# A three-layer graph convolution: two teams for three in the second layer, four blocks more fetched by index, a longer landing ring

## The chip, the core and the metric

The kernel runs on one core of one Trainium2 chip. The metric is the device time of one execution in microseconds, median of several runs. A core has five engines with a queue each: TensorE (PE in the profile, its weight loads PEld), VectorE (DVE), ScalarE (ACT), GpSimd (POOL) and SyncE (SP, here used for starting DMAs). An engine works through its queue in order.

## The reference

A graph has N = 6250 nodes with 256 features and 100,000 edges, sorted by destination. Three graph-convolution layers follow each other, then a residual and a layer norm:

```python
deg  = segment_sum(1, dst with self loops);  dinv = rsqrt(deg)
h = x
for W, b in ((W1, b1), (W2, b2), (W3, b3)):       # 256 -> 512 -> 512 -> 256
    t   = h @ W
    agg = segment_sum(t[src] * (dinv[src] * dinv[dst]), dst)
    h   = relu(agg + b)
return layernorm(x + h)
```

## The kernel before, in words

The nodes lie in 50 blocks of 125 (`NB`, `Q`). For each layer a table in HBM holds one row per node, scaled by `dinv` (`tab0`, `tab1`, `tab2`; rows of the second are 512 floats, 2 KB). A block's aggregate is the sum over the edges that end in it, and the kernel has two ways to it.

*By fetched rows.* The block's edges stand in 16 groups of 128 (`KF`), and an edge list of leftovers serves ten blocks together (`rest`). For a group, GpSimd starts an indirect DMA that fetches 128 rows (`gather`); TensorE multiplies them with a 0/1 matrix made by VectorE (`more_hots`). For two passes of fast matmuls each fetched row is split into a rounded high part (a cast on ScalarE) and the rest (a subtraction on VectorE).

*By count matrices.* The first layer makes, for 29 blocks, a matrix of 125 x 6250 edge counts and keeps it in HBM (`kept`). A block's aggregate is then 50 products of a count piece with a block of the table. In the first and third layer these stand under `L1398`; in the second layer four blocks form a team (`teams`): the table is streamed from HBM in pairs of blocks, split into two parts, and multiplied with count pieces that are 500 columns wide. One turn of the inner loop is a pair, two matmuls of 500 columns (L1004). A team takes 50 x 4 pairs.

`layer(i, ...)` writes out one layer by hand: its loop runs over `chunk`, one fetched group per turn (called a step below). In each step it issues the gather of group c, the cast of group c - `hi_lag`, the subtraction of group c - `lo_lag`, the two matmuls of group c - `lag`, and then lets other coroutines go on: `going` holds the dense stages behind finished blocks (`after2`, `hidden`: L1417, L1504, L1512, L1524, L1539 and so on), `fixed` holds the extras: `teams`, `in_advance` (the third layer's first products, for three blocks) and `home`. A coroutine that yields n is called again n steps later. The order in each engine's queue is just the order of this code.

In the second layer the 12 team blocks are blocks 0 to 11; blocks 12 to 49 are fetched, 38 x 16 groups and 4 of leftovers, 612 steps. Fetched rows land in `wide_rows`, eight places of 2 KB in `room` and `back`, one of them for leftovers. Split rows lie in nine places and three lent ones (`loaned`) in the big tile `all_parts`; until the teams are done, the part of `all_parts` behind block `HOME` serves as the teams' working space (`carved`): stream ring, count pieces, both parts. Finished blocks of the third table whose place in `parts` lies there go only to HBM (`waiting`), and `home` reloads them after the teams, in runs of up to four. `returning` is set six units before the teams end; from then on the loans go back and the lags shrink. `PACE` sets how the teams' pairs follow from step 9 (`EAGER`) on.

Of the kernel before, what the change touches and what calls it, by code (L numbers as in the profile page):

```python
# [10 lines left out]
F32 = mybir.dt.float32  # L11
# [15 lines left out]
Q = 125  # L27
KF = 16
# [10 lines left out]
SPLIT_ROWS = (12, 9, 20)  # L39
LOANED = 3  # L40
EAGER = 9
PACE = 24
LANDING = 8
AT_ONCE = 3
RETURN = 6
SHORT = 6
# [9 lines left out]
BOTH_LAG = 5  # L56
SPLIT = ((0, 0, BOTH_LAG), (1, 2, 8), (0, 0, 10))
EXTRAS_AFTER = (3, 6, 9, 11, 13, 15, 17)
TEAM = 4
TEAMS = 3  # L60
HOME = 17
TAIL = 4
MANY = 29
BEGUN = 3
SOONER = -2
ADVANCE = (0, 12, 17, 22, 27, 32, 37)
AT_HOME = 2
ALONE = 2
# [339 lines left out]
def sorted_path(ctx: ExitStack, tc: tile.TileContext, x, edges, starts, found, wts, biases, room, late, out):  # L408
# [347 lines left out]
    x_rows = [room[:Q, 3 * MW:3 * MW + C], scratch[:Q, MW:MW + C]]  # L756
    turn = 0

# [141 lines left out]

    RING = 3
    streamed = [carved(2 * HID).bitcast(F32).rearrange("p (b c) -> p b c", b=2) for _ in range(RING)]
# [5 lines left out]
    loaned = [wide_tail[:, cut - n * 2 * HID:][:, :2 * HID] for n in range(LOANED, 0, -1)]  # L908
    on_loan = []
    team_banks = [accs[2], mat_bank, mm_bank, tr_bank]  # L910
    couple, waiting = [], []
# [3 lines left out]
    def teams(groups):  # L915
# [71 lines left out]
        for u, (g, k) in enumerate(units):  # L987
            if u == len(units) - RETURN:
                returning = now
            if u % 2:  # L990
                load((u + 1) // 2 + RING - 1)
            for n in range(TEAM):
                if k == 0:
                    yield from take(f"team{n}", 1)
                if k == NB - 1 and n == 0:
                    while held.get("tz", 0):
                        yield 1
                    held["tz"] = TEAM // 2
                if 1 <= n < 3:
                    half(u + 2, n - 1)  # L1000
                if k % PIECE == 2 and u + PIECE < len(units):
                    piece(*divmod(g * CUTS + k // PIECE + 1, CUTS), n)
                for h in range(2):
                    nc.tensor.matmul(team_banks[n][:, :TEAM * Q], lhsT=both_parts[u % 3][:, h * HID + n * P:h * HID + (n + 1) * P],  # L1004
                                     rhs=team_pieces[(g * CUTS + k // PIECE) % 2][:, k % PIECE, :],
                                     start=(k == h == 0), stop=(k == NB - 1 and h == 1))
                if k == NB - 1:
                    team_ended[0](scaled(g, n))
                pairs_done += 1
                if in_layer == 0 and pairs_done % 3 or in_layer == 1 and (pairs_done % PACE if now >= EAGER else pairs_done % 3 == 0):  # L1010
                    yield 1
# [14 lines left out]
    def in_advance():  # L1026
# [36 lines left out]
        for u, (m, k0) in enumerate(units):  # L1063
# [3 lines left out]
            for k in range(PIECE):  # L1067
# [3 lines left out]
                sent += 1  # L1071
                if sent % (2 if u < AT_HOME * BEGUN else AT_ONCE):
                    yield 1

    def home():
# [9 lines left out]
        for run in runs:  # L1085
            b, e = run[0], run[-1] + 1
            by_rows(nc.sync, parts[:, b:e].bitcast(F32), tables[2][b * Q:e * Q, :].rearrange("(b p) c -> p b c", p=Q))
            final.update((k, now + LANDING) for k in range(b, e))
            yield 4

# [65 lines left out]
    def layer(i, width, gathered, dense, after, rows, first=0, spacing=1.0, extras=(), carried=None):  # L1156
# [6 lines left out]

        nonlocal turn, finished, now, in_layer, products
        in_layer = i
# [101 lines left out]
        def of_both(c):  # L1267

            n, b, _ = items[c]
            return i == 2 or i == 0 and (n * GRP if b is None else b) >= BOTH_FROM  # L1270

        def halved(c):

# [8 lines left out]
        def gather(c):  # L1282
            nonlocal turn
            n, b, j = items[c]
# [12 lines left out]
            else:  # L1297
                row, at = rows[turn % len(rows)], src[:, b, j:j + 1]
                (landed if i == 1 else split_rows)[c] = row
                turn += 1  # L1300
            nc.gpsimd.indirect_dma_start(out=row, out_offset=None, in_=table,  # L1301
# [43 lines left out]
        with tc.manual_schedule():  # L1345
            more_hots()
            to_sum = 0
            for chunk in range(total + (SHORT if i == 1 else lag)):
# [3 lines left out]
                if i == 1:  # L1352
                    lag = SPLIT[i][2] if returning is None else max(SHORT, SPLIT[i][2] - (chunk - returning) // 2)
                if chunk < total:
                    gather(chunk)
                if halved(chunk - hi_lag):
                    halves = split_rows[chunk - hi_lag] = split.popleft()
                    if i == 1 and halves in loaned:
                        on_loan.append(halves)
                    nc.scalar.copy(halves[:, :width], landed[chunk - hi_lag])  # L1360
                if halved(chunk - lo_lag):
                    halves = split_rows[chunk - lo_lag]
                    nc.vector.tensor_sub(halves[:, width:], landed.pop(chunk - lo_lag), halves[:, :width].bitcast(F32))  # L1363
                while to_sum <= chunk - lag:
# [57 lines left out]
    def after1(b, acc, bank):  # L1422
# [28 lines left out]
        nc.scalar.activation(y, y, AF.Relu, scale=dinv[:, b:b + 1])  # L1451
        by_rows(nc.sync, y, tables[1][b * Q:(b + 1) * Q, :], store=True)

# [186 lines left out]
    def last_weights():  # L1640
# [9 lines left out]
    own_row = two.enter_context(tc.tile_pool(name="sown_row", bufs=1)).tile([P, HID], F32, name="own_row")[:Q]  # L1650
    layer(1, HID, every[TEAM * TEAMS:], [], after2, wide_rows,
          extras=[(5, last_weights()), (0, team_steps), (20, in_advance()), (20, home())])
    there[:] = [0]
# [193 lines left out]
```

## Time and profile before

| | |
|---|---|
| Time, median of 3 runs | 2064.19 us (2059.42 to 2065.3) |
| Profiled execution | 2065.68 us, its span 2063.9 us |
| Mean granted TensorE clock | 0.984 |
| HBM traffic | 459.56 MB read, 73.87 MB written, 258 GB/s over the span |
| First gather of the second layer | at 709.7 us |
| Last gather of the second layer | at 1616.9 us |
| First gathers of the third layer | just before 1650 us |

The profile's lines name a source line (L1301 is the gather in `layer`), the engine, the operation, the tiles written and read, the count, the busy time and mean duration, and then the engine's idle time just before such instructions with the releaser that ended most of it. The releaser "issue" means that the profile shows nothing that was waited for. Matmuls overlap each other, so that the mean of one is longer than its share of the engine's time; the shares are read from busy time by stage. A gather's duration is the time in which GpSimd makes the DMA; the rows land later. Fetched rows in the second layer have `room` or `back` as their tile (after the change also `parts`); in the third layer, `halves`.

### The profile page before, as it was taken

How to read it: one execution, taken by the hardware profiler on the slowest of the kernel's cores; microseconds unless marked ns; L12 is line 12 of the kernel's file. 1: busy time of each engine (PE TensorE's matmuls, PEld its weight loads, DVE VectorE, ACT ScalarE, POOL GpSimd, SP SyncE). 2: the span in 40 equal slices, each digit the busy share in tenths (PEclk: the TensorE clock that was granted, in tenths of full speed). 3: DMA queues.
4: the chain of work that ended last, by engine and by line, in shares of the span. 5: the costliest groups of instructions: out<-in, count | busy, mean ns of one | idle time of the engine just before them, and what ended most of it. 6: DMA issues, size and time to landing. Idle time of an engine off the chain costs nothing.

```text
span 2063.9 us, 29139 instructions
## 1 busy us (share of the span) xinstructions
PE 1925.4 (93%) x8679; PEld 1517.8 (74%) x8679; DVE 1377.3 (67%) x2443; ACT 1278.4 (62%) x2255; POOL 1383.6 (67%) x1425
## 2 busy tenths in 40 slices
PE   4499999999999689999999989999989999999997
PEld 3377777777777467778888768887768777778776
DVE  6877888888882277777676676766756445444444
ACT  2566777787875366666676666666656455555553
POOL 2466777766777377677777676766657277777775
PEclk9999999999999899999999999999999999999999
DMA  7898999999999999999999998989897599999997
GB/s 172 247 293 227 265 264 259 273 262 255 276 273 250 258 267 262 264 261 267 261 258 263 264 261 250 268 252 258 248 272 234 151 286 290 290 298 295 294 285 204
DMA packets 266078, 535.53 MB, mean 259 GB/s; under 512 B 44363, under 2 KB 80328, under 8 KB 265910
## 3 DMA queue, kind: packets, MB, share of 16 engines
q0 software_dynamic: 155280, 355.58, 63.0%
q1 hardware_dynamic: 97348, 168.71, 30.5%
q10 hardware_dynamic: 13282, 9.30, 1.7%
q8 instruction: 70, 1.15, 0.2%
q14 instruction: 98, 0.80, 0.1%
HBM read 459.56 MB, written 73.87 MB: 258 GB/s over the span
## 4 chain that ended last, share of the span: by engine, by line
PE 62%; DMA 13%; issue 9%; POOL 8%; DVE 3%; ACT 2%; SPq 0%; POOLq 0%; DVEq 0%; ACTq 0%
PE sacc L1329 12%; DMA room<-tab,ssrc 6%; PE win_ps L1398 6%; PE str L1398 5%; PE smm L1398 5%; PE sacc L1398 5%; PE mat_ps L1398 5%; POOL room L1301 5%; PE win_ps L1504 4%; PE win_ps L1524 2%; POOL back L1301 2%; DMA back<-tab,ssrc 2%; PE sacc L1443 2%; DMA parts<-tab 2%; PE sacc L877 1%
## 5 line engine op out<-in xcount | busy, mean ns | idle before, releaser
L1301 POOL DMA_INDIRECT room<-tab,ssrc x442 | 456.3, 1032 | 201.6 <-issue 82.5
L1329 PE MATMUL sacc<-halves,shot 128*125 128x512 f32 x1524 | 517.2, 400 | 10.3 <-ACT halves L1360 3.9
L1254 ACT CAST piece<-room 125x625 fp32r<-125x625 uint8 x492 | 350.7, 720 | 186.7 <-PE win_ps L1398 52.7
L1301 POOL DMA_INDIRECT halves<-both,ssrc x384 | 360.7, 939 | 144.3 <-issue 42.7
L1301 POOL DMA_INDIRECT halves<-tab,ssrc x320 | 302.9, 947 | 97.8 <-issue 22.0
L1329 PEld LDWEIGHTS sacc<-halves,shot 128*125 128x125 f32 x1524 | 284.9, 187 | 87.0 <-DVE halves L1363 8.2
L810 DVE TENSOR_TENSOR back<-near_cols,slots 128x625 bf16<-128x625 f32 (+2 forms) x435 | 325.0, 803 | 29.7 <-PE sacc L877 13.0
L1363 DVE TENSOR_TENSOR halves<-room,halves 128x512 fp32r<-128x512 f32 x334 | 227.1, 693 | 126.0 <-ACT halves L1360 124.2
L1245 DVE TENSOR_TENSOR shot<-near_cols,sdlo 128x500 fp32r<-128x500 f32 x366 | 245.0, 670 | 93.0 <-PE sacc L1329 87.5
L1301 POOL DMA_INDIRECT back<-tab,ssrc x230 | 233.2, 1014 | 109.2 <-DVE halves L1363 33.8
L1360 ACT CAST halves<-room 128x512 fp32r<-128x512 f32 x334 | 201.8, 620 | 145.3 <-DMA room<-tab,ssrc 119.6
L1504 PE MATMUL win_ps<-back,w_sb 128*128 128x250 f32 x768 | 186.4, 387 | 6.5 <-ACT back L1481 5.3
L1504 PEld LDWEIGHTS win_ps<-back,w_sb 128*128 128x128 f32 x768 | 150.4, 197 | 31.2 <-ACT back L1481 7.1
L1398 PE MATMUL smm<-parts,piece 125*125 125x512 f32 x565 | 165.9, 408 | 2.1 <-DVE parts L1554 1.2
L1398 PE MATMUL win_ps<-parts,piece 125*125 125x512 f32 x550 | 156.9, 403 | 0.0
L1398 PE MATMUL str<-parts,piece 125*125 125x512 f32 x515 | 149.5, 408 | 0.9 <-ACT piece L1254 0.9
L877 PEld LDWEIGHTS <-back 128*125 128x125 bf16 x725 | 96.0, 138 | 73.7 <-issue 23.2
L1398 PE MATMUL sacc<-parts,piece 125*125 125x512 f32 x450 | 147.4, 431 | 0.9 <-ACT piece L1254 0.9
L839 ACT CAST room<-sacc 125x500 uint8<-125x500 f32 (+1 forms) x155 | 107.6, 712 | 56.4 <-PE sacc L877 42.0
L1363 DVE TENSOR_TENSOR halves<-back,halves 128x512 fp32r<-128x512 f32 x136 | 93.2, 691 | 62.0 <-ACT halves L1360 61.6
L961 DVE TENSOR_TENSOR parts<-parts 125x512 fp32r<-125x512 f32 x150 | 103.2, 688 | 38.1 <-ACT parts L959 37.9
L1398 PE MATMUL mat_ps<-parts,piece 125*125 125x512 f32 x415 | 121.2, 408 | 0.4 <-ACT piece L1254 0.4
(353 smaller groups left out, 3470.9 us busy)
## 6 DMA issues: line engine op xcount, KB each, us to landing
parts<-tab SPq DMA_DIRECT2D x75, 448.0 KB
kept<-room SPq DMA_DIRECT2D x29, 683.6 KB
room<-kept SPq DMA_DIRECT2D x27, 683.6 KB
tab<-st SPq DMA_DIRECT2D x51, 224.0 KB
both<-parts SPq DMA_DIRECT2D x10, 1120.0 KB
own_row<-tab SPq DMA_DIRECT2D x38, 224.0 KB
parts<-kept SPq DMA_DIRECT2D x60, 136.7 KB
room<-tab,ssrc POOLq DMA_INDIRECT x442, 6.6
```

Of the source, the lines that this page charges most:

```text
L810: nc.vector.tensor_tensor(out, near_cols[:, :shape[2]].unsqueeze(1).to_broadcast(shape), numbers.unsqueeze(2).to_broadcast(shape), op=ALU. ...
L839: nc.scalar.copy(place[:, :, u * G:(u + len(ms)) * G].rearrange("p k (t r) -> p t k r", r=G), counted_in[:Q, :len(ms) * 256].rearrange("p ...
L877: nc.tensor.matmul(bank[:Q, len(pair) * 256:][:, :G * NB], lhsT=hot_lo, rhs=hot_key, start=True, stop=True)
L961: nc.vector.tensor_sub(to[:, HID:], row, to[:, :HID].bitcast(F32))
L1245: nc.vector.tensor_tensor(hot[:, :n], near_cols[:, :Q].unsqueeze(1).to_broadcast([P, n, Q]), dlo.rearrange("p b j -> p (b j)")[:, at:at + ...
L1254: nc.scalar.copy(piece[:, :n], made_or_read[:, at:at + n, :])
L1301: nc.gpsimd.indirect_dma_start(out=row, out_offset=None, in_=table, in_offset=bass.IndirectOffsetOnAxis(ap=at, axis=0))
L1329: nc.tensor.matmul(acc[:Q, :size], lhsT=hot, rhs=row[:, c0:c0 + size], start=(i != 0 and k == c0 == 0), stop=(k == KF and c0 + size == row ...
L1360: nc.scalar.copy(halves[:, :width], landed[chunk - hi_lag])
L1363: nc.vector.tensor_sub(halves[:, width:], landed.pop(chunk - lo_lag), halves[:, :width].bitcast(F32))
L1398: nc.tensor.matmul(acc_d[:Q], lhsT=got[p][:, n, :], rhs=parts[:, k], start=begins and not (i == 2 and m < BEGUN), stop=ends)
L1504: nc.tensor.matmul(h_ps[:, f, :], lhsT=w2_sb[:, k, (f2 + f) * P:(f2 + f + 1) * P], rhs=zt[:, k, :], start=(k == 0), stop=(k == KH - 1))
```

## The change

Two teams take blocks 0 to 7, and blocks 8 to 49 are fetched: 42 x 16 groups and 5 of leftovers, 677 steps. From step 9 on the teams do two pairs in three steps (`PACE` 2), where they did 25 pairs in 24. Fetched rows land in a ring of 14 places with the one for leftovers: six half-size places (`lent`) are taken from the teams' space, which begins at block 13 now, and the stream ring there has two places for three. At `returning` the six places leave the ring. The cast and the subtraction stand four and five steps behind the gather (before: one and two; the first few groups five and six), the matmuls eleven steps (before: eight), all shrinking after `returning`. `home` reloads a run every eight steps for four, `in_advance` sends one product per step, for three in two steps, after its first three pieces, and covers rows 8 to 42 of the third table for 0 to 4 and 12 to 41. The last block of the first layer is stored from ScalarE's queue.

```diff
+LENT = 6
-PACE = 24
+PACE = 2
...
-AT_ONCE = 3
...
-SPLIT = ((0, 0, BOTH_LAG), (1, 2, 8), (0, 0, 10))
+SPLIT = ((0, 0, BOTH_LAG), (4, 5, 11), (0, 0, 10))
...
-TEAMS = 3
-HOME = 17
+TEAMS = 2
+HOME = 13
...
+SLOW_START = 5
-ADVANCE = (0, 12, 17, 22, 27, 32, 37)
-AT_HOME = 2
+ADVANCE = (8, 13, 18, 23, 28, 33, 38)
+AT_HOME = 1
...
-    RING = 3
+    RING = 2
...
+    carved(LENT * HID)
+    lent = [wide_tail[:, cut - n * HID:][:, :HID].bitcast(F32) for n in range(LENT, 0, -1)]
...
-            if u % 2:
-                load((u + 1) // 2 + RING - 1)
+            if u % 2 == 0:
+                load(u // 2 + RING)
...
-                if in_layer == 0 and pairs_done % 3 or in_layer == 1 and (pairs_done % PACE if now >= EAGER else pairs_done % 3 == 0):
+                if in_layer == 1 and now >= EAGER:
+                    yield PACE if pairs_done % PACE else 1
+                elif (pairs_done % 3 == 0) == in_layer:
                     yield 1
...
-                if sent % (2 if u < AT_HOME * BEGUN else AT_ONCE):
+                if sent % 2 or u >= AT_HOME * BEGUN:
                     yield 1
...
-            yield 4
+            yield 8
...
+        def later(c):
+
+            usual = hi_lag if returning is None else max(1, hi_lag - (now - returning) // 2)
+            return max(usual, SLOW_START - c // SLOW_START)
...
-                row, at = rows[turn % len(rows)], src[:, b, j:j + 1]
+                if i == 1 and returning is not None:
+                    while rows[0] in lent:
+                        rows.pop(0)
+                row, at = rows.pop(0), src[:, b, j:j + 1]
                 (landed if i == 1 else split_rows)[c] = row
-                turn += 1
+                rows.append(row)
...
-                    lag = SPLIT[i][2] if returning is None else max(SHORT, SPLIT[i][2] - (chunk - returning) // 2)
+                    lag = SPLIT[i][2] if returning is None else max(SHORT, SPLIT[i][2] - (chunk - returning))
...
-        by_rows(nc.sync, y, tables[1][b * Q:(b + 1) * Q, :], store=True)
+        by_rows(nc.scalar if b == NB - 1 else nc.sync, y, tables[1][b * Q:(b + 1) * Q, :], store=True)
...
-    layer(1, HID, every[TEAM * TEAMS:], [], after2, wide_rows,
-          extras=[(5, last_weights()), (0, team_steps), (20, in_advance()), (20, home())])
+    layer(1, HID, every[TEAM * TEAMS:], [], after2, wide_rows + lent,
+          extras=[(KF, last_weights()), (0, team_steps), (20, in_advance()), (20, home())])
```

The line numbers of the changed kernel are a few higher: the gather is L1312, the cast and subtraction L1372 and L1377, the fetched groups' matmuls L1340, the teams' L1006, the dense stages L1519 and L1539.

On TensorE, in the middle of the second layer, the queue before reads as follows; `sacc<-halves` are a fetched group's two matmuls, `<-parts 128x500` a team pair, `win_ps` a dense stage.

```order
L1329 MATMUL sacc_892<-halves_6029,shot_853 125x512 x2
L1504 MATMUL win_ps<-back,w_sb 128x250 x4
L1004 MATMUL smm<-parts 128x500 x2
L1329 MATMUL sacc_892<-halves_6030,shot_853 125x512 x2
L1504 MATMUL win_ps<-back,w_sb 128x250 x4
L1004 MATMUL str<-parts 128x500 x2
L1329 MATMUL sacc_892<-halves_6031,shot_853 125x512 x2
L1004 MATMUL sacc_893<-parts 128x500 x2
```

The same place after the change:

```order
L1340 MATMUL sacc_892<-halves_6032,shot_851 125x512 x2
L1340 MATMUL sacc_892<-halves_6033,shot_852 125x512 x2
L1519 MATMUL win_ps<-back,w_sb 128x250 x4
L1006 MATMUL str<-parts 128x500 x2
L1340 MATMUL sacc_892<-parts,shot_852 125x512 x2
L1519 MATMUL win_ps<-back,w_sb 128x250 x4
L1006 MATMUL sacc_893<-parts 128x500 x2
L1340 MATMUL sacc_892<-parts,shot_852 125x512 x4
```

Each fetched group had a team pair behind it; now every third group has none, so that two groups follow each other.

On GpSimd, at the start of the second layer, the queue before (`rest` is the fetch of leftovers, a count behind a row stands for gathers in a row):

```order
L1301 DMA room<-tab_169,rest 128x512
L1301 DMA room<-tab_169,ssrc 128x512 x4
L1301 DMA back<-tab_169,ssrc 128x512 x2
L1301 DMA room<-tab_169,ssrc 128x512 x5
L1301 DMA back<-tab_169,ssrc 128x512 x2
```

and after:

```order
L1312 DMA room<-tab_169,rest 128x512
L1312 DMA room<-tab_169,ssrc 128x512 x5
L1312 DMA back<-tab_169,ssrc 128x512 x2
L1312 DMA parts<-tab_169,ssrc 128x512 x6
L1312 DMA room<-tab_169,ssrc 128x512 x5
```

The ring of seven places became thirteen, six of them in `parts`.

On SP, after the teams, where blocks of the third table are reloaded (`4x512` is a run of four), before:

```order
L86 DMA d<-kept 13x625
L86 DMA parts<-tab_170 112x4x512
L86 DMA parts<-tab_170 13x4x512
L86 DMA parts<-tab_170 112x4x512
L86 DMA parts<-tab_170 13x4x512
L86 DMA own_row<-tab_169 112x512
L86 DMA own_row<-tab_169 13x512
L86 DMA parts<-tab_170 112x4x512
```

and after:

```order
L87 DMA parts<-tab_170 112x4x512
L87 DMA parts<-tab_170 13x4x512
L87 DMA own_row<-tab_169 112x512
L87 DMA own_row<-tab_169 13x512
L85 DMA tab_170<-parts 112x2x512
L85 DMA tab_170<-parts 13x2x512
L87 DMA parts<-tab_170 112x4x512
L87 DMA parts<-tab_170 13x4x512
```

The load of a block's own rows (`own_row`), which stood behind up to four runs' reloads, now comes after at most two.

More of the change, by code (lines that the diff above doesn't have):

```diff
@@ L756, in sorted_path @@
     x_rows = [room[:Q, 3 * MW:3 * MW + C], scratch[:Q, MW:MW + C]]
-    turn = 0
     onehot = ctx.enter_context(tc.tile_pool(name="sonehot", bufs=1))
@@ L1156, in layer @@
     def layer(i, width, gathered, dense, after, rows, first=0, spacing=1.0, extras=(), carried=None):
-        nonlocal turn, finished, now, in_layer, products
+        nonlocal finished, now, in_layer, products
         in_layer = i
@@ L1282, in gather @@
         def gather(c):
-            nonlocal turn
             n, b, j = items[c]
@@ L1346, in layer @@
             more_hots()
-            to_sum = 0
+            to_sum = highs = lows = 0
             for chunk in range(total + (SHORT if i == 1 else lag)):
@@ L1352, in layer @@
                 if i == 1:
-                    lag = SPLIT[i][2] if returning is None else max(SHORT, SPLIT[i][2] - (chunk - returning) // 2)
+                    lag = SPLIT[i][2] if returning is None else max(SHORT, SPLIT[i][2] - (chunk - returning))
                 if chunk < total:
                     gather(chunk)
[L1356 to L1363, printed above, removed]
+                while i == 1 and highs < total and highs + later(highs) <= chunk:
+                    if halved(highs):
+                        halves = split_rows[highs] = split.popleft()
+                        if halves in loaned:
+                            on_loan.append(halves)
+                        nc.scalar.copy(halves[:, :width], landed[highs])
+                    highs += 1
+                while i == 1 and lows < total and lows + later(lows) < chunk:
+                    if halved(lows):
+                        halves = split_rows[lows]
+                        nc.vector.tensor_sub(halves[:, width:], landed.pop(lows), halves[:, :width].bitcast(F32))
+                    lows += 1
                 while to_sum <= chunk - lag:
```

## The prediction

> **What bounds the kernel now.** I read the page first (busy line, costliest groups), then stages, groups and waits of the second layer, then single rows. A step is one pass of the layer's loop, with one gather; the pitch is the time between gathers.
>
> ```profile
> span 2063.9 us, 29139 instructions
> PE 1925.4 (93%) x8679; PEld 1517.8 (74%) x8679; DVE 1377.3 (67%) x2443; ACT 1278.4 (62%) x2255; POOL 1383.6 (67%) x1425
> parts<-tab SPq DMA_DIRECT2D x75, 448.0 KB
> parts<-kept SPq DMA_DIRECT2D x60, 136.7 KB
> ```
>
> ```profile
> core 0: us, PE busy (x) PEld busy (x) DVE busy (x) ACT busy (x) POOL busy (x), PEclk, DMA share, GB/s
> 709.70:779.20 69.50, 54.18 (x217) 40.31 (x216) 46.27 (x74) 43.34 (x77) 49.69 (x50) 0.93 0.94 277
> 779.20:1454.70 675.50, 655.85 (x2899) 539.67 (x2898) 485.95 (x773) 446.29 (x822) 477.92 (x459) 0.98 0.92 260
> 1454.70:1489.10 34.40, 34.17 (x155) 28.00 (x154) 23.82 (x38) 19.55 (x37) 22.67 (x23) 1.00 0.86 246
> 1489.10:1541.50 52.40, 41.31 (x170) 32.68 (x171) 28.13 (x44) 27.29 (x49) 27.68 (x28) 0.93 1.02 273
> 1541.50:1617.90 76.40, 75.80 (x344) 63.50 (x343) 46.92 (x75) 45.62 (x86) 52.27 (x52) 0.98 0.78 226
> 1617.90:1650.00 32.10, 29.73 (x163) 24.44 (x162) 12.66 (x26) 15.67 (x31) 1.27 (x2) 1.00 0.43 118
> 1650.00:2063.90 413.90, 400.84 (x1726) 317.67 (x1724) 199.31 (x485) 209.66 (x333) 303.55 (x321) 0.99 1.13 280
> ```
>
> The columns are busy time and count by engine. The second layer's 612 gathers run from 709.7 to 1617.9, 908.2 us. I cut that at steps 50, 509 (the teams ask for their loans back), 532 (teams done) and 560 (the last reload). In the long stage TensorE is busy 97%, 655.85 / 459 = 1.43 us of a step of 675.5 / 459 = 1.472 us, in 6.3 instructions of 0.226 us. TensorE bounds it. GpSimd comes next.
>
> ```profile
> L1301 POOL DMA_INDIRECT room<-tab,ssrc x326 | 341.9, 1049 | 139.2 <-issue 61.5 <-DVE halves L1363 49.0 <-DVE parts L1363 16.8
> L1301 POOL DMA_INDIRECT back<-tab,ssrc x130 | 133.2, 1025 | 57.5 <-issue 22.9 <-DVE halves L1363 19.7 <-DVE parts L1363 7.2
> L1363 DVE TENSOR_TENSOR halves<-room,halves 128x512 fp32r<-128x512 f32 x238 | 162.5, 693 | 90.1 <-ACT halves L1360 88.8 <-PE sacc L1329 0.9
> L1360 ACT CAST halves<-room 128x512 fp32r<-128x512 f32 x239 | 145.1, 620 | 102.8 <-DMA room<-tab,ssrc 101.2 <-DVE halves L1363 0.8 <-PE sacc L1329 0.2
> 839.51 9.09 DMA room<-tab,ssrc
> ```
>
> Of 1.472 us a gather takes 477.92 / 459 = 1.04 and 0.43 lies between gathers, part of it waits for the subtraction (L1363) that frees a landing place. The last row is one of the pieces where the chain runs through a landing: seven places against some 9 us to land and a split behind them. So TensorE's limit, 1.43, and the ring's, (9.1 + 0.62 + 0.69) / 7 = 1.49, lie together.
>
> **What a gather costs when nothing holds it.** The first two rows are of the last layer, the next two are first and last of 34 gathers late in the second layer (33 pitches, 1.283 us each), the others show gathers and subtractions that meet.
>
> ```profile
> 1800.03 0.94 POOL L1301 DMA_INDIRECT halves<-tab,ssrc  x1 [0.30 <-PE win_ps L1398]
> 1801.27 0.94 POOL L1301 DMA_INDIRECT halves<-tab,ssrc  x1 [0.30 <-issue]
> 1557.05 0.95 POOL L1301 DMA_INDIRECT room<-tab,ssrc  x1 [0.30 <-issue]
> 1599.40 0.95 POOL L1301 DMA_INDIRECT room<-tab,ssrc  x1 [0.30 <-issue]
> 1007.02 1.50 POOL L1301 DMA_INDIRECT room<-tab,ssrc  x1 [0.30 <-issue]
> 1008.82 0.94 POOL L1301 DMA_INDIRECT room<-tab,ssrc  x1 [0.30 <-issue]
> 1018.60 1.44 POOL L1301 DMA_INDIRECT room<-tab,ssrc  x1 [0.30 <-issue]
> 1007.01 0.68 DVE L1363 TENSOR_TENSOR halves<-room,halves 128x512 fp32r<-128x512 f32 x1
> 1007.61 0.69 DVE L1363 TENSOR_TENSOR halves<-back,halves 128x512 fp32r<-128x512 f32 x1
> 1017.93 1.28 DVE L1363 TENSOR_TENSOR parts<-back,parts 128x512 fp32r<-128x512 f32 x2
> ```
>
> The floor is 0.94 + 0.30 = 1.245 us. A gather that begins during a subtraction of two SBUF tensors ends late (1.50, 1.44), one beside none takes 0.94. VectorE makes such a subtraction per step, and one more per four team pairs (L961): 0.26 per step now. So gathers cost 1.04 while the teams run and 52.27 / 52 = 1.005 after them.
>
> The Trainium skill ("SBUF — State Buffer", Who interferes with whom) says that a VectorE instruction with two SBUF inputs contends with a GpSimd instruction that reads SBUF and not with one that only writes it, and infers from an older probe that making descriptors is of the second kind. By that inference nothing would hold a gather and the sum below would take 1.245 where it takes 1.34, some 47 us less. The rows above show the holding, so the trace goes with the first half of the rule, which speaks against the change.
>
> **The change, part by part.** *Teams.* 200 pairs of team products go, 400 matmuls of 0.226 us: -90 us of TensorE. Four blocks more are gathered: 4 x 34 matmuls, +31 us. Net -59 us; the dense stages behind a block stay. *Steps.* 42 x 16 + 5 = 677 gathers for 38 x 16 + 4 = 612: 65 more, on GpSimd 65 x 1.245 = 81 us at least. *Pace.* Some 54 pairs are done by step 9 as now; then two pairs in three steps for 25 in 24, so the teams end near 9 + 346 x 1.5 = step 528, now 532. TensorE's need per step falls by 0.37 pairs x 2 x 0.226 and the teams' dense share, 0.04: 1.43 to 1.22 us. *Ring of 14 (one for the rests), splits four steps on.* Thirteen landing places let GpSimd run some eight steps ahead of VectorE; (9.1 + 1.3) / 13 = 0.80 us, no limit. No engine gets a new wait: ScalarE's casts of rows stand four steps later, so that the teams' casts queued behind them wait less for landings (101.2 us now). *DMA.* A pair costs 500 KB / 8 streamed and 153 KB / 10 of counts, 78 KB: 383 KB per step (260 GB/s x 1.472) becomes 353, at 1.34 us 263 GB/s. That is today's load, not more.
>
> So GpSimd sets the pitch. I cut its 677 steps as above.
>
> A, steps 0 to 492 (loans called back): 1.245, plus 0.05 for the subtraction of each step (1.283 less the floor is 0.04, 1.005 less 0.945 is 0.06), plus 0.03 for 0.167 team subtractions per step (0.26 cost 1.04 - 1.00 = 0.04), plus 0.015 for waits that the ring still leaves: 1.34 us, 659 us. Ends: 1.283 (631) and 1.40 (689), if gathers that run on end are met oftener.
>
> B, 492 to 528: six landing places go back, seven are left, the teams still run. Today's stage of that kind takes 34.4 / 23 = 1.496, TensorE-bound; between that and 1.283 I take 1.42: 51 us (46 to 54).
>
> C, 528 to 584: 25 blocks of the third table come home, as now, but eight steps apart. Now:
>
> ```profile
> 1541.56 1.15 POOL L1301 DMA_INDIRECT room<-tab,ssrc  x1 [10.79 <-DVE halves L1363]
> 1538.72 0.72 ACT L1340 ACTIVATE own_row<-own_row,sdinv 125x512 f32<-125x512 f32 x1 [9.93 <-DMA own_row<-tab]
> ```
>
> ScalarE waited 9.93 us for a row queued on SP behind the reloads, and all behind it. That stage moved 273 GB/s. Now 56 steps x 294 KB + 6.4 MB + 1 MB of counts = 24 MB; at 273 GB/s 88 us, or 80 if 2 MB of it land later, during D: I take 84 (1.50 per step; ends 75 and 95). The 10 us wait should shrink, since two reloads and not four stand between own rows.
>
> D, 584 to 677: 93 steps with one early product per step (now 1.5); TensorE needs 1.2 us, not the 75.80 of 76.40 of now. The pitch is that of the 34 gathers, with some waits 1.30: 121 us (119 to 130).
>
> Sum: 659 + 51 + 84 + 121 = 915 us against 908.2: +7 us. A saves some 61 us on the first 492 steps (745.0 x 492 / 509 = 720 now); the steps behind them, 185 for 120, take 256 us for 188 and give it back. Behind the last gather nothing changes: last products, the store, 32 us.
>
> *At one price each.* The last block's store on ScalarE's queue: the store was issued as its activation ended, so nothing to -1 us. A stream ring of two: loads go out two units ahead (8 pairs, 16 us) for three (17 us now), nothing. The split's slow start removes part of this wait at the layer's start:
>
> ```profile
> 719.78 1.51 PE L1004 MATMUL sacc<-parts 125*128 125x500 f32 x2 [9.47 <-ACT parts L959]
> 709.73 0.96 POOL L1301 DMA_INDIRECT room<-tab,rest  x1 [22.43 <-DMA parts<-tab]
> ```
>
> It gives TensorE time, while gathers set the pitch: nothing; if TensorE were the bound, -9. HOME 13 lets the teams' first loads go five products later: +1 us, hidden by the smaller first load. ADVANCE takes other rows but as many (35 of three blocks); the last layer, TensorE busy 400.84 of 413.90, stays.
>
> The profiled execution took 2065.7 us (span 2063.9), 1.5 above the median of 2064.2; on the median +7 is 2071.
>
> **Rivals.** *Faster: gathers run almost free.* Free-running gathers could settle between the subtractions, since both have the same period; then A goes at the 1.283 of the 34 gathers (those too had one subtraction per step): 631 us, total -21, 2043. For it: those rows. Against it: they had no team subtractions beside them, and the long stage's cost 1.04 on average. It decides from a pitch below (908 - 256) / 492 = 1.325 us. At the floor of 1.245, where nothing holds a gather, A would take 613 us, -39 in all, 2025; that has 0.03 of this rival's chance. (It is what the inference in the Trainium skill, same section, would give.) *No change: the reloads cost nothing extra.* C at 1.34 takes 75 us, total -2, 2062. For it: half the rate of reloads. Against: 24 MB in 75 us is 320 GB/s, above every stage here. *Much slower: the pitch stays.* If landing or TensorE holds the steps at 1.472 with the ring at 14, A takes 724 us, +72, 2136. Against: TensorE's need falls by 0.21 us a step and DMA's by 30 KB. *Slower: gathers held oftener*, pitch 1.40: +37, 2101.
>
> **How the numbers follow.** No change is within 0.3% (6 us), about what a measurement can tell here. Forecast 0.48, with its own range of 2062 to 2089; faster 0.28; no change 0.12; held oftener 0.08; pitch stays 0.04. Slower by over 6 us: 0.7 of the forecast, 0.34, and the last two, 0.46. Same: a quarter of the forecast and most of the third case, 0.22. Faster: the second case and the lower ends of the first and third, 0.32. For the range I leave out the last rival and the outer halves of faster and held oftener: 2045 to 2097.
>
> **What would show it.** Right: in the long stage TensorE below 92%, gathers' idle near 0.30 and their pitch 1.32 to 1.36; the 677 gathers 905 to 930 us long; reload stage near 270 GB/s with steps of 1.4 to 1.6. Wrong: pitch below 1.32 there, or above 1.40; gathers of 0.95 beside subtractions; waits for landings in the ring of 14; a last layer of other than 410 us.

## The result, and the profile after

The kernel after takes 2083.52 us (median of 6 runs, 2081.46 to 2085.16), the kernel before 2065.76 in the same runs (2059.42 to 2069.95). The ratio is 1.0078, interval 1.0064 to 1.0091: slower by 0.8%. The profiled execution took 2083.65 us, 2081.9 of it between the first and the last instruction.

The busy line and the stages of the kernel after, in the page's form and cut as before (start of the second layer, long stage, loans gone, reloads, rest, tail, last layer):

```profile
span 2081.9 us, 28671 instructions
PE 1905.4 (92%) x8431; PEld 1479.5 (71%) x8431; DVE 1399.1 (67%) x2475; ACT 1274.2 (61%) x2238; POOL 1452.7 (70%) x1490
```

```profile
core 0: us, PE busy (x) PEld busy (x) DVE busy (x) ACT busy (x) POOL busy (x), PEclk, DMA share, GB/s
708.40:774.90 66.50, 54.06 (x194) 37.13 (x192) 45.16 (x71) 40.30 (x71) 51.20 (x50) 0.92 0.93 276
774.90:1371.20 596.30, 556.07 (x2387) 446.52 (x2388) 437.38 (x697) 388.49 (x713) 460.39 (x443) 0.97 0.89 258
1371.20:1422.20 51.00, 45.68 (x187) 35.69 (x186) 34.45 (x55) 28.29 (x50) 36.46 (x36) 0.90 0.84 236
1422.20:1511.60 89.40, 77.89 (x315) 60.63 (x314) 52.23 (x83) 46.73 (x84) 56.53 (x57) 0.92 1.00 275
1511.60:1638.60 127.00, 113.59 (x484) 90.53 (x482) 84.00 (x133) 75.91 (x139) 94.68 (x93) 0.95 0.75 221
1638.60:1668.00 29.40, 25.56 (x133) 20.05 (x134) 12.34 (x26) 14.21 (x29) 0.86 (x2) 0.94 0.50 140
1668.00:2081.90 413.90, 400.26 (x1724) 318.45 (x1722) 199.06 (x483) 209.29 (x333) 303.48 (x322) 0.99 1.12 280
```

What to see: the last layer is the same 413.90 us. The whole difference lies in the second layer, whose 677 gathers run from 708.46 to 1638.6: some 930 us against 908 (the other parts are some 4 us shorter together). In the long stage a step takes 596.30 / 443 = 1.346 us (1.472 before), and TensorE is busy for 93% of it, at a granted clock of 0.97. So it does wait now. The stages behind the loans, 51.0 + 89.4 + 127.0 = 267 us for 185 steps, took 189.5 us for 120 steps (from step 492, at 1428.28 us of the profile before).

The gathers of the long stage, by destination (busy, mean ns of one; idle before them, and what ended it):

```profile
L1312 POOL DMA_INDIRECT parts<-tab,ssrc x203 | 211.6, 1042 | 62.2 <-issue 36.5 <-DMA room<-tab,ssrc 6.7 <-DVE halves L1377 6.1
L1312 POOL DMA_INDIRECT room<-tab,ssrc x170 | 178.2, 1048 | 52.7 <-issue 29.9 <-DMA parts<-tab,ssrc 10.4 <-DVE halves L1377 6.1
```

The idle time before a gather is 62.2 / 203 = 0.306 and 52.7 / 170 = 0.310 us, the 0.30 that stands between any two gathers. GpSimd waits for hardly any landing place. It works almost without a break, and one gather is 1.04 us long on the mean, not 0.945.

Which gathers are long can be read from single rows. A subtraction of two SBUF tensors, a gather that begins while it runs, and what follows on both engines:

```profile
842.03 0.69 DVE L1377 TENSOR_TENSOR halves<-room,halves 128x512 fp32r<-128x512 f32 x1 [2.67 <-ACT halves L1372]
842.25 1.29 POOL L1312 DMA_INDIRECT parts<-tab,ssrc  x1 [0.30 <-issue]
842.64 0.68 DVE L963 TENSOR_TENSOR parts<-parts 125x512 fp32r<-125x512 f32 x1
843.84 0.95 POOL L1312 DMA_INDIRECT parts<-tab,ssrc  x1 [0.30 <-DMA back<-tab,ssrc]
```

The subtraction ends at 842.72 and the gather at 843.54, 0.82 us later. The second subtraction begins within the gather and holds it no further. Counted over the 443 gathers of this stage: 84 began with 0.2 to 0.6 us of such a subtraction left, and all 84 took over 1.0 us and ended 0.82 us behind its end on the mean. Of 95 that began with less than 0.15 us of it left none took over 1.0 us, and the 163 that began beside none took 0.95 on the mean. So the price of a gather depends on where in a subtraction it begins.

The reload stage and the one behind it: a gather and an own-row scaling with the wait ahead of them, two gathers of the rest (the second is the last of the layer), and what GpSimd waited for from 1558 to 1638:

```profile
1452.94 1.15 POOL L1312 DMA_INDIRECT room<-tab,ssrc  x1 [6.46 <-DVE halves L1377]
1450.57 0.72 ACT L1351 ACTIVATE own_row<-own_row,sdinv 125x512 f32<-125x512 f32 x1 [6.03 <-DMA own_row<-tab]
1567.95 0.95 POOL L1312 DMA_INDIRECT back<-tab,ssrc  x1 [1.82 <-DVE halves L1377]
1637.70 0.95 POOL L1312 DMA_INDIRECT room<-tab,ssrc  x1 [0.30 <-DVE halves L1377]
```

```profile
POOL room L1312 <- DVE halves L1377: 4.7, 7, 1.8
POOL back L1312 <- DVE halves L1377: 2.7, 4, 1.8
```

ScalarE's wait for an own row is 6.03 us where it was 9.93. In the last stage the ring has seven places again, and GpSimd waits for subtractions again, eleven times, 7.4 us in all, of which 0.30 each stand between any two gathers.

### The profile page after: what moved, and what is told of

It is laid out like the page before. It is cut to its first block, busy times and chain, and to the rows that moved or that the text cites. A ratio compares the mean times of both kernels' runs of the same rounds, so it can differ in the third digit from the quotient of the medians.

```text
span 2081.9 us, 28671 instructions
## 1 busy us (share of the span) xinstructions
PE 1905.4 (92%) x8431; PEld 1479.5 (71%) x8431; DVE 1399.1 (67%) x2475; ACT 1274.2 (61%) x2238; POOL 1452.7 (70%) x1490
## 4 chain that ended last, share of the span: by engine, by line
PE 57%; DMA 19%; issue 8%; POOL 7%; DVE 4%; ACT 3%; POOLq 0%; ACTq 0%; SPq 0%; DVEq 0%
PE sacc L1340 10%; DMA room<-tab,ssrc 9%; DMA parts<-tab,ssrc 6%; PE smm L1413 6%; PE win_ps L1413 6%; PE str L1413 5%; PE sacc L1413 5%; PE mat_ps L1413 5%; PE win_ps L1519 4%; DMA back<-tab,ssrc 3%; POOL room L1312 3%; POOL parts L1312 2%; PE sacc L1458 2%; PE sacc L877 1%; PE win_ps L1539 1%
## 5 line engine op out<-in xcount | busy, mean ns | idle before, releaser
L1340 PE MATMUL sacc<-halves,shot 128*125 128x512 f32 x1689 | 578.0, 413 | 36.8 <-ACT halves L1372 21.5
L1312 POOL DMA_INDIRECT halves<-both,ssrc x384 | 360.9, 940 | 141.5 <-issue 42.2
L1312 POOL DMA_INDIRECT room<-tab,ssrc x329 | 340.8, 1036 | 121.5 <-issue 60.0
L1340 PEld LDWEIGHTS sacc<-halves,shot 128*125 128x125 f32 x1689 | 319.4, 190 | 139.2 <-ACT halves L1372 31.4
L1312 POOL DMA_INDIRECT halves<-tab,ssrc x320 | 302.4, 945 | 97.7 <-issue 20.5
L1249 DVE TENSOR_TENSOR shot<-near_cols,sdlo 128x500 fp32r<-128x500 f32 x383 | 256.2, 670 | 92.6 <-PE sacc L1340 87.8
L1312 POOL DMA_INDIRECT parts<-tab,ssrc x223 | 232.8, 1044 | 68.3 <-issue 40.5
L1377 DVE TENSOR_TENSOR halves<-room,halves 128x512 fp32r<-128x512 f32 x269 | 181.7, 692 | 117.5 <-ACT halves L1372 111.2
L1372 ACT CAST halves<-room 128x512 fp32r<-128x512 f32 x269 | 162.4, 620 | 137.7 <-DMA room<-tab,ssrc 115.8
L1312 POOL DMA_INDIRECT back<-tab,ssrc x184 | 184.6, 1003 | 73.5 <-issue 34.1
L1519 PE MATMUL win_ps<-back,w_sb 128*128 128x250 f32 x768 | 192.9, 397 | 19.5 <-ACT back L1496 13.4
L1519 PEld LDWEIGHTS win_ps<-back,w_sb 128*128 128x128 f32 x768 | 152.8, 201 | 49.6 <-ACT back L1496 17.3
L1377 DVE TENSOR_TENSOR halves<-parts,halves 128x512 fp32r<-128x512 f32 x164 | 110.0, 691 | 41.7 <-ACT halves L1372 39.1
L1372 ACT CAST halves<-parts 128x512 fp32r<-128x512 f32 x164 | 98.1, 618 | 54.4 <-DMA parts<-tab,ssrc 43.8
```

The costliest lines, as they stand in the source:

```text
L1249: nc.vector.tensor_tensor(hot[:, :n], near_cols[:, :Q].unsqueeze(1).to_broadcast([P, n, Q]), dlo.rearrange("p b j -> p (b j)")[:, at:at + ...
L1340: nc.tensor.matmul(acc[:Q, :size], lhsT=hot, rhs=row[:, c0:c0 + size], start=(i != 0 and k == c0 == 0), stop=(k == KF and c0 + size == row ...
L1372: nc.scalar.copy(halves[:, :width], landed[highs])
L1377: nc.vector.tensor_sub(halves[:, width:], landed.pop(lows), halves[:, :width].bitcast(F32))
L1519: nc.tensor.matmul(h_ps[:, f, :], lhsT=w2_sb[:, k, (f2 + f) * P:(f2 + f + 1) * P], rhs=zt[:, k, :], start=(k == 0), stop=(k == KH - 1))
```

## The experiments

The theory: GpSimd sets the pitch of the long stage, and a gather is held by subtractions that read two SBUF tensors. Rivals: the transfers (landings) hold it; or TensorE does. A second question is which part of the change earns and which costs: the ring of 14 with its late splits, or two teams in place of three.

Four groups of runs were made, each with the kernel before beside it on the same chip. It took 2292.06, 2287.34 and 2260.39 us on the chips of the first, second and fourth group, and 2063.76 on that of the third. So only the third group stands beside the numbers above (the kernel after itself was not run on that chip). The other three are called slow chips here, and their runs are read within their group.

**One SBUF input.** Both subtractions take a PSUM operand in the place of the high part (the low parts are then not the reference's). VectorE no longer waits for ScalarE's cast there either.

```diff
-nc.vector.tensor_sub(to[:, HID:], row, to[:, :HID].bitcast(F32))
+one_input(to[:, HID:], row)          # row minus near_cols (PSUM)
-nc.vector.tensor_sub(halves[:, width:], landed.pop(lows), halves[:, :width].bitcast(F32))
+one_input(halves[:, width:], landed.pop(lows))
```

> The changed kernel, with the low part of each fetched row and of each streamed row of the second layer subtracted from a PSUM tensor of column numbers in place of the rounded high part: the VectorE instruction keeps its size and place, but reads one SBUF tensor and not two. The low parts' values are therefore wrong. Theory (subtractions of two SBUF tensors hold the gathers, and the gathers set the pitch): in the long stage gathers take 0.95 us for 1.045, the pitch falls from 1.347 to 1.25-1.26, the 492 steps before the loans return take 617 us for 663, and the whole 2020 to 2040 us. Rival (DMA or landings set the pitch at some 260 GB/s): gathers shorten but their idle grows by as much, pitch 1.33-1.35, whole 2075 to 2085. Between them, if DMA gives out at the 275 GB/s of the reload stage: pitch near 1.29, whole near 2050.

Measured: 2377.91 us, ratio 1.0373 (1.0307 to 1.0439). Gathers were short, but on this chip the time didn't fall. The kernel after was not run on this chip. The same edit on a second one:

> The changed kernel with one SBUF input in the subtractions (low parts' values wrong), a second time, since the first chip ran every kernel 11% slower, the last layer included, and its transfers, not the gathers, held the pitch. On a chip where the kernel before takes about 2066 us: theory (subtractions of two SBUF tensors hold the gathers, and the gathers set the pitch) pitch of the long stage 1.25-1.26 for 1.347, whole 2020 to 2040 us; if DMA gives out on the way, pitch near 1.29, 2050; rival (DMA sets the pitch) 2075 to 2085. On a chip where the kernel before takes about 2290 us: about 1.035 times that, as before.

Measured: 2379.19, ratio 1.0398 (1.0348 to 1.0448). (The "first chip" of that expectation is the slow one of the first group.) The kernel after on the same chip:

> The changed kernel itself beside the others, to have all on one chip. On a chip where the kernel before takes about 2066 us 2080 to 2087. On one where it takes about 2290: if transfers set the pitch there, the 2.4 MB more in the second layer alone are some 10 us and the ratio stays under 1.01; if what counts is the number of gathers with their fixed cost, 677 for 612, the ratio is 1.03 to 1.04.

Measured: 2373.36, ratio 1.0383 (1.0336 to 1.0429). On a slow chip the edit is worth nothing. The third group had a chip like the first:

> The changed kernel with one SBUF input in the subtractions (low parts' values wrong), a third time, for a chip where the kernel before takes about 2066 us. There: theory (held gathers set the pitch) pitch of the long stage 1.25-1.26 us for 1.347, whole 2020 to 2040; DMA giving out on the way, pitch near 1.29, 2050; rival (DMA sets the pitch) 2075 to 2085. Where the kernel before takes about 2290 us: 1.04 times that.

Measured: 2032.41 us, ratio 0.9861 (0.9832 to 0.989). Its long and reload stages, its gathers in the long stage, and the chain of that stage by line; the last fence is the same line of the kernel after:

```profile
768.80:1326.00 557.20, 540.24 (x2401) 445.81 (x2401) 429.55 (x704) 381.75 (x714) 419.74 (x442) 0.98 0.94 277
1375.50:1463.50 88.00, 75.81 (x307) 58.13 (x307) 51.84 (x83) 46.49 (x83) 52.98 (x57) 0.92 0.99 275
```

```profile
L1317 POOL DMA_INDIRECT parts<-tab,ssrc x202 | 192.6, 953 | 62.6 <-issue 15.5 <-DVE halves L796 7.9 <-ACT halves L1377 7.8
L1317 POOL DMA_INDIRECT room<-tab,ssrc x170 | 161.0, 947 | 52.5 <-issue 13.7 <-DMA parts<-tab,ssrc 8.1 <-ACT halves L1377 6.4
```

```profile
by line: PE sacc L1345 26.8%; PE win_ps L1524 17.2%; PE win_ps L1544 8.7%; DMA room<-tab,ssrc 6.5%; DMA parts<-tab,ssrc 5.6%; DMA back<-tab,ssrc 5.0%; PE sacc L1011 4.5%; PE str L1011 4.3%; PE mat_ps L1011 4.1%; PE smm L1011 4.0%; issue 3.5
```

```profile
by line: DMA room<-tab,ssrc 18.7%; DMA parts<-tab,ssrc 18.4%; issue 12.2%; PE sacc L1340 9.9%; PE win_ps L1519 8.5%; POOL parts L1312 6.6%; DMA back<-tab,ssrc 4.9%; POOL room L1312 4.5%; PE win_ps L1539 2.9%; PE mat_ps L1006 1.7%; PE sacc L
```

The gather falls from 1.04 to 0.95 us, idle stays 0.31, and the pitch falls with the gather, from 1.346 to 557.20 / 442 = 1.261. In the kernel after the chain runs through gathers and landings. With the short gathers it is on TensorE, busy 97%. GpSimd has hardly any slack there either, since its gathers still stand 0.31 us apart, and 0.95 + 0.31 is the pitch: TensorE, which needs 540.24 / 442 = 1.22, lies close behind. The transfers as bound fall: the same kind of load moves at 277 GB/s here, where it moved at 258. TensorE as bound falls for the kernel after, since its work is the same in both. One thing isn't separated: VectorE's freedom from ScalarE's cast came with the edit (its subtraction itself takes 0.68 us for 0.69). But GpSimd waited for hardly any place before it, so there was little for that to free.

The same edit in the kernel before:

> The kernel before with the same substitution (low parts' values wrong). Theory (there TensorE, with the ring of seven close behind it, sets the pitch and not the gathers): gathers take 0.95 us for 1.04, but their idle grows, pitch 1.44 to 1.47 for 1.472, whole 2045 to 2065 us. Rival (the gathers' duration sets the pitch there too): pitch falls by the full 0.09 us, 612 steps, whole 2005 to 2015.

Measured: 2292.77, ratio 1.0001 (0.9971 to 1.0031), gathers of 0.95 us. Shorter gathers are worth nothing there, but this was a slow chip, where they were worth nothing in the kernel after either, so it says nothing of the chip like the first.

**Which subtractions.** The edit in the fetched rows' subtraction alone, the teams' left as it is:

> The changed kernel with one SBUF input in the subtraction of the fetched rows alone; the teams' streamed rows are subtracted as before (low parts of the fetched rows are wrong). It tells apart what the two kinds of subtraction cost the gathers: both together cost 1.347 - 1.260 = 0.087 us per step. Prediction's split (0.05 fetched, 0.03 team): pitch of the long stage 1.285-1.30, whole 2043 to 2052 on a chip where the kernel before takes about 2064 us. Rival (each subtraction costs alike, 1 to 0.167): pitch 1.27, whole 2035 to 2041. Other rival (the teams' cost most): pitch 1.31 or more, whole above 2058.

Measured: 2363.34, ratio 1.0436 (1.0399 to 1.0472), on a slow chip. The time tells nothing, but the gathers' durations can be compared across slow chips. Gathers alone in the long stage (the last columns are clock, DMA share, GB/s): the kernel after, fetched rows only, both:

```profile
853.10:1552.60 699.50, 459.38 (x442) 0.90 0.77 220
849.10:1546.60 697.50, 428.22 (x443) 0.90 0.76 221
856.80:1562.50 705.70, 421.47 (x443) 0.89 0.76 218
```

A gather takes 1.039, 0.967 and 0.951 us. So the fetched rows' subtractions cost 0.07 us a step and the teams' 0.015: with 0.167 of the latter per step, 0.07 and 0.09 per subtraction, nearly alike. These are prices on a slow chip, where steps are longer (1.58 us).

**Three teams with the ring.** The kernel after with the teams, their pace and the reloads' spacing of before. The ring of 14, late splits, slow start and the smaller parts stay.

```diff
-PACE = 2
+PACE = 24
-TEAMS = 2
+TEAMS = 3
-ADVANCE = (8, 13, 18, 23, 28, 33, 38)
-AT_HOME = 1
+ADVANCE = (0, 12, 17, 22, 27, 32, 37)
+AT_HOME = 2
...
-            yield 8
+            yield 4
```

> The changed kernel with three teams again: ring of 14, splits four and five steps on and products eleven, stream ring of two, but 12 team blocks, the old pace of 25 pairs in 24 steps, the old early rows and reloads every four steps. Theory (the loss comes from the 65 more gathers at a pitch that gathers set; the ring by itself takes waits away): pitch of the long stage falls from 1.472 to TensorE's need of 1.43-1.44, whole 2040 to 2055 us, faster than both kernels. Rival (the ring itself costs, by more transfers in flight or by the later splits): whole 2070 to 2090. Third (landings were no part of the old pitch): 2060 to 2068.

Measured: 2320.14, ratio 1.0115 (1.0049 to 1.0181).

> Three teams with the ring of 14 and the late splits, a second time for the same reason. On a chip where the kernel before takes about 2066 us: theory (the ring takes waits away, the 65 more gathers cost) pitch of the long stage 1.43-1.44 for 1.472, whole 2040 to 2055; rival (the ring itself costs) 2070 to 2090, as on the slow chip, where it was 1.2% above the kernel before; third (landings were no part of the old pitch) 2060 to 2068.

Measured: 2311.61, ratio 1.01 (1.0065 to 1.0136). On slow chips this part costs 1%. On the chip like the first:

> Three teams with the ring of 14 and the late splits, a third time, for a chip where the kernel before takes about 2066 us. There: theory (the ring takes waits away, the 65 more gathers cost) pitch of the long stage 1.43-1.44 us for 1.472, whole 2040 to 2055; rival (the ring itself costs) 2070 to 2090; third (landings were no part of the old pitch) 2060 to 2068. Where the kernel before takes about 2290 us: 1.01 times that.

Measured: 2034.13 us (2032.95 to 2042.83), ratio 0.9873 (0.9845 to 0.9902). It leaves nothing out, and it beats both kernels. Its long stage, its reload stage, and an own row's scaling there:

```profile
774.40:1393.60 619.20, 614.51 (x2778) 513.28 (x2777) 461.22 (x739) 420.63 (x784) 465.83 (x442) 1.00 0.95 273
1450.00:1544.90 94.90, 84.48 (x363) 68.83 (x362) 54.65 (x87) 52.10 (x95) 57.36 (x56) 0.93 0.96 265
1505.42 0.72 ACT L1349 ACTIVATE own_row<-own_row,sdinv 125x512 f32<-125x512 f32 x1 [9.18 <-DMA own_row<-tab]
```

The ring takes the pitch from 1.472 to 619.20 / 442 = 1.401, with TensorE busy 99% at a granted clock of 1.00. In the kernel before, 83 of the 459 gaps between gathers of the long stage are over 0.4 us, here 20 of 442. So the ring and what goes with it are worth some 30 us (2063.76 to 2034.13). Two teams for three, with what goes with them, then cost some 49 (2034.13 to 2083.52; the two times are from two chips, on which the kernel before agrees to 2 us; by the ratios it is 42). In the gathers: this kernel's first 492 steps take 686.3 us and its last 120 take 191.1; the kernel after takes 662.7 and, for 185, 267.5. The two teams save 24 us and then spend 76.

**Two teams without the ring.**

```diff
-SPLIT = ((0, 0, BOTH_LAG), (4, 5, 11), (0, 0, 10))
+SPLIT = ((0, 0, BOTH_LAG), (1, 2, 8), (0, 0, 10))
-SLOW_START = 5
+SLOW_START = 1
-layer(1, HID, every[TEAM * TEAMS:], [], after2, wide_rows + lent,
+layer(1, HID, every[TEAM * TEAMS:], [], after2, wide_rows,
```

> The changed kernel with the old ring of seven and the rests' place, casts and subtractions one and two steps behind the gather and products eight: two teams without the ring. Theory (the ring is what lets gathers run on end): gathers wait for subtractions again, pitch of the long stage 1.40 to 1.47 for 1.347, whole 2110 to 2145 us. Rival (with TensorE's need at 1.22 us the ring of seven is long enough, since few transfers queue): pitch within 0.03 of 1.347, whole 2080 to 2098.

Measured: 2369.11, ratio 1.0346 (1.0271 to 1.042).

> Two teams with the old ring of seven and the old distances, a second time, for a chip where the kernel before takes about 2064 us. If the ring's gain is the same as with three teams (30 us): 2113. Theory (with two teams GpSimd and not TensorE is the bound, so the ring counts for more): pitch of the long stage 1.41 to 1.47 for 1.347, whole 2118 to 2145. Rival (at TensorE's lower need the short ring is long enough): pitch up to 1.37, whole 2083 to 2098.

Measured: 2344.98, ratio 1.0368 (1.0331 to 1.0404). Both on slow chips, where the kernel after has 1.0383: there the ring is worth nothing with two teams. What it is worth with two teams on a chip like the first wasn't tried.

**Own row earlier.** The three-team kernel above; the condition under which an own row is loaded reads `else 5` in place of `else KF - LATE`.

```diff
-            if i == 1 and j == (3 if b == NB - 1 else KF - LATE):
+            if i == 1 and j == (3 if b == NB - 1 else 5):
```

> Three teams with the ring of 14, and each block's own rows asked for after its sixth product and not after its eleventh. On a chip where the kernel before takes about 2064 us: theory (ScalarE's 9.2 us wait for own rows behind the reloads holds the whole reload stage, 94.9 us for 56 steps) stage 83 to 87 us, whole 2022 to 2028, the best of all; rival (the reload stage is bounded by the bytes that it moves) the wait for own rows goes and waits for landings take its place, whole 2030 to 2037.

Measured: 2285.86, ratio 1.0108 (1.0073 to 1.0143), against 1.01 without the edit. The waits for own rows fell from 17.2 to 8.7 us, the reload stage did not (97.4 for 95.3 us). Inconclusive, on a slow chip.

**What the slow chips show.** The kernel after there: two stretches of its long stage, 18 and 14 us long, and four weight loads at the end of the second:

```profile
1050.00:1068.00 18.00, 17.68 (x81) 14.33 (x80) 14.74 (x24) 13.45 (x25) 11.62 (x12) 1.00 0.74 212
1068.60:1082.50 13.90, 4.70 (x9) 2.27 (x9) 3.32 (x6) 1.85 (x3) 9.00 (x9) 0.63 1.00 294
```

```profile
1080.01 0.28 PEld L1340 LDWEIGHTS sacc<-parts,shot 128*125 128x125 f32 x1 [2.50 <-issue]
1081.40 0.28 PEld L1340 LDWEIGHTS sacc<-parts,shot 128*125 128x125 f32 x1 [1.11 <-issue]
1082.11 0.28 PEld L1340 LDWEIGHTS sacc<-parts,shot 128*125 128x125 f32 x1 [0.42 <-issue]
1082.82 0.29 PEld L1340 LDWEIGHTS sacc<-parts,shot 128*125 128x125 f32 x1 [0.43 <-issue]
```

TensorE goes from 81 matmuls in 18 us to 9 in 14, while GpSimd goes on gathering and the DMA engines are full. Its starts lie 1.39, 0.71 and 0.71 us apart, one and two times 0.7, and no wait is shown. I counted, from the first gather of the second layer on, the stretches in which six matmuls in a row took over 6 us until the next one started: 5 of 37 us together in the kernel after on the first chip, and 17 of 204 us in it on the slow one. Kernels with three teams have 9 to 13 on slow chips (87 to 136 us), those with two teams 16 to 24 (149 to 258 us). So two-team kernels meet it more, which goes with their ratios of 1.035 to 1.044 there against 1.00 to 1.0115. The kernel after is 289 us longer there: 72 ahead of the second layer, 138 in its gathers, 75 in the last layer. The last layer, whose work is the same in all the kernels, has a single such stretch, so the stretches aren't all of it. What makes TensorE start so slowly stays open. Transfers as the bound, which some expectations above supposed, are not borne out: the DMA engines are busy 0.77 of the long stage for 220 GB/s there, 0.89 for 258 on the first chip, the same time per byte and more time free. The landings of gathers aren't matched in those traces either, so part of what they call "issue" may be landings.

## Why the prediction was right, and where its terms were off

The forecast was 2071 and slower; 2083.5 is inside its range, 12 us over its centre. Its mechanism, TensorE work that is saved and paid back by 65 more gathers that GpSimd sets the pitch of, is what the runs show. Its sign was less sure than that: it is the small rest of two large terms, -61 and +68 in the forecast, -56 and +78 measured. The terms of three stages were 4 to 6 us low each, and one of them was read from a miscount. By its steps:

- *GpSimd sets the pitch of the long stage.* Shown, by the short gathers on the chip like the first: pitch and gather fall together, down to 1.26, where TensorE's need of 1.22 is close.
- *Stage A, 1.34 us.* Measured 662.7 us, 1.347: 4 us over. The sum of the two holding terms, 0.05 + 0.03, was nearly right: the pitch fell by 0.085 and the gather by 0.09 when both went. Its split was not borne out: 0.07 and 0.015 on the slow chips. The 0.05 came from gathers that met fewer subtractions: of the 52 behind the reloads in the kernel before 20 began while one ran, of the 443 in the long stage after 280. The 0.015 for waits of the ring was nearly absent (idle 0.306).
- *Stage B, 51 us.* Measured 51.05.
- *Stage C, 84 us.* Measured 89.3, 5 us over. The bytes were right: 275 GB/s for 89.4 us are 24.6 MB, so nothing of the forecast's 24 MB was left for later. The choice of letting 2 MB land later was wrong, and the bound by bytes, 88 us, was the better value. That bytes hold this stage isn't shown by a run of its own, though short gathers left it at 88.0 us and 275 GB/s. That halving the reloads' rate would shorten the own-row wait was right in part, 9.93 to 6.03.
- *Stage D, 1.30 us.* Measured some 127 us for 93 steps, 1.366: 6 us over. Its pitch was read from "34 gathers" at 1.283 in the kernel before. They are 32: from the first, at 1557.05, up to the last, at 1599.40, 31 pitches of 42.35 / 31 = 1.366 us. The row has the gathers of that stretch without the last one (length, busy time and count, then clock, DMA share, GB/s):

```profile
1557.04:1599.39 42.35, 31.14 (x31) 1.00 0.77 229
```

So the rows that the forecast went by showed the very pitch that stage D then had. Of the 0.12 above the floor of 1.245 a half is the gathers' length (31.14 / 31 = 1.005) and a half waits for places, in a ring of seven as in stage D, where the gathers were 94.68 / 93 = 1.018 us long. With the short gathers, on the chip like the first, that stage took 120.7 us.

- *Nothing behind the last gather.* Nearly: from there to the third layer's first gather 29.5 us for 31.6.
- *TensorE's need, 1.43 us before.* Over-read. The three-team kernel with the ring needs 614.51 / 442 = 1.39: its granted clock is 1.00 in that stage, where it was 0.98, and an instruction takes 0.221 us, not 0.226. *The old ring's limit, 1.49,* came from one landing of 9.1 us. The median of all landings in `room` is 6.6 us by the page of the profile before, which gives (6.6 + 1.31) / 7 = 1.13, so seven places held the gathers only at long landings. The prediction took the new ring for no limit, rightly, but gave it no gain of its own. The three-team run shows that the ring and what goes with it are worth 30 us by themselves, 32 of the 56 us that the change gains in its first 492 steps (718.6 before, 686.3, 662.7).
- *TensorE below 92% in the long stage* was wrong by a point: 93%.

Of the rivals, the faster one (a pitch of 1.283, gathers that run free of the subtractions) is refuted: gathers stayed at 1.04. Its chance of 0.28 rested on the miscount, since at 1.366 the rows named for it speak against it. A pitch of 1.40 or 1.472 is refuted by 1.347, and reloads that cost nothing extra by 89.3 us for 75. The landings as bound are refuted by 277 GB/s with short gathers. The rule weighed there, the Trainium skill's "SBUF — State Buffer" (Who interferes with whom), infers that making descriptors isn't held by a VectorE instruction whose only use of what the two engines share is to read a second SBUF tensor; the runs show indirect gathers held by subtractions of two SBUF tensors, by 0.09 us on the mean, so the measurement decides against the inference.

## What to carry to other kernels

When a change swaps work of the bounding engine for work of another, price the other one as it runs in company: the last layer's gather cost 0.945 us, the one beside subtractions 1.04, and over 677 steps that difference, 64 us, is more than the result. Try the parts of such a change apart: here a deeper ring with later splits, which only removed pauses, was worth 30 us, and the exchange of work packed with it cost more than that. Busy time per step at a granted clock of 0.98 overstated TensorE's need here (1.43 for 1.39), so let the pauses go first and then see what is left to move. And count the rows from which a pitch is read: 32 gathers taken for 34 made 1.366 look like 1.283, and a term and a rival were built on that.

## What the runs showed of the hardware

- An indirect gather is held by VectorE's subtraction of two SBUF tensors: 1.04 us on the mean in the long stage, 0.95 when one operand comes from PSUM. A gather that begins with 0.2 to 0.6 us of such a subtraction left ends 0.82 us behind its end (84 of 84); one that is under way when the subtraction begins is hardly held (113 that began beside none and met one later took 0.95).
- One and the same kernel took 2063.76 us on one chip and 2260.39 to 2292.06 on three others. On those TensorE has stretches of 6 to 21 us in which its instructions start some 0.7 us or a multiple of it apart. The ring with three teams gains 1.3% on the one and costs 1% on the others; one SBUF input in the kernel after gains 45 us by the ratios, 51 by the times, on the one and nothing on the others. A per cent may have the other sign on another chip.
